# Masked attention and an int8 linear layer on one core: PSUM tiles taken by threes, v and q in other portions, the second-last linear layer moved behind the last scores

## The chip, the core and the metric

The kernel runs on 1 of the 8 cores of a Trainium2 chip. The metric is device time in microseconds (us); the time before is 2547.27 us, the median of 3 runs (2547.04 to 2548.92). TensorE is called PE, VectorE DVE, ScalarE ACT, GpSimd POOL and SyncE SP, as in the profile. PE works out of SBUF into PSUM; DVE and ACT read PSUM; POOL works on SBUF alone. Each engine runs its instructions in the order of the program and waits on semaphores of the others.

## The reference, cut to what matters

```python
# x: (8, 512, 1024) f32, mask: (8, 1024); 16 heads of 32 channels
Q, K, V = (proj(Wq), proj(Wk), proj(Wv))          # each (B, H, T, Dh) from x (B, C, T)
att = jnp.einsum('bhqd,bhkd->bhqk', Q, K) * (1.0 / math.sqrt(Dh))
att = att + b[0]
att = att * m + (1.0 - m) * NEG_INF
att = jax.nn.softmax(att, axis=-1)
y = jnp.einsum('bhqk,bhkd->bhqd', att, V)         # back to (B, C, T)
...
q, in_scale = per_token_quant_int8(y)             # one scale for each row of T values
acc = jnp.einsum('bsk,nk->bsn', q, weight, preferred_element_type=jnp.int32)
out = acc.astype(jnp.float32) * in_scale * w_scale[:, 0] + bias
return x + out.astype(jnp.float16)
```

So each batch has 16 heads with 1024 x 1024 scores, and the linear layer sees each channel's 1024 values over T as one row.

## The kernel before

**Groups, halves, steps, pairs.** The 8 x 16 heads are taken as 32 groups `i` of four heads (128 channels; four groups to a batch). A group has two halves of 512 queries (`X = 2i + h`), and a half has 8 steps of 128 keys (`s`, 512 in all). The main loop runs over pairs `n` of two steps: 8 pairs to a group (`p` = 0 to 7), 256 in all, and five pairs ahead of them (`n` = -5 to -1, `i` = -1, `p` = 3 to 7) that only prepare. All five engines are scheduled by hand: an engine's order is the order of the calls.

**What a step does.** `scores` (L408) writes the scores of four heads, keys by queries, into two PSUM tiles of two banks each: L419 puts in the negated maximum of each query (`shift`), L424 adds k times q. ACT takes the exponential (L433) into a tile `e` of SBUF, of which there are three. `product` (L451, its matmuls L458) multiplies `e` with v into one bank (`ps_av`); after 8 steps ACT copies that to `y` (L468). `add_up` (L438) sums the `e` of a half on POOL (L445), and ones-matmuls turn the sum into the denominators (`half_denominators` L478, `add_rows` L472). For the last 12 steps (`s >= ON_ARRAY`) there is no sum on POOL: `last_denominators` (L488) feeds every `e` to the ones-matmuls (L474) as it comes, and a copy (L504) brings the result to SBUF. `normalise` (L506) takes four reciprocals (L511) and one product (L514).

**Maxima.** The maximum of each query over its unmasked keys has to be known before the scores that are exponentiated. `maxima` (L335) computes the scores of 128 queries against 1024 keys of one head into a PSUM tile of two banks, from `stacks` in which q and k stand as high and low halves (L345), and DVE reduces it (L376). Each pair of steps works off four such units, five pairs ahead; the first eight units of all are `first_maxima` (L354), from the unsplit q and k. `split_tops` on POOL (L393 to L397) and a DMA transpose on SP (L402) make `shift` of eight units' worth of maxima and more: once per half, at the start of the pair before the half's first scores are due.

**PSUM.** Eight banks: two tiles of two banks under `ps_s`, one of two banks under `ps_m`, one bank `ps_av`, one bank `ps_job`. Scores take both `ps_s` tiles in every step. `maxima_bank` (L330) lets unit `k` use `ps_s` where `k % 4` is 1 or 2 and `ps_m` otherwise, so that the units follow each other as m, s, s, m, m, s, s, m.

**Jobs.** Beside that, `job` (L690) hands every pair a list of pieces that use the one bank `ps_job`: `project` (L199) makes q or k of a half of a coming group, as a rule as 8 matmuls of 256 columns (two quarters by four chunks `c` of 128 input channels); where `(i + 2) % 4 == 0`, and `p` = 4, as 4 matmuls of 512 columns, so that the last q of a batch gives its chunks of `x` free one by one. `project_v` (L281) makes v in quarters of two key tiles; `linear` (L622) is the int8 layer, half an output at a time. `evict` (L230) splits q and k into high and low with two ACT instructions and, by way of `later`, one of DVE at the end of the pair. The main loop (L818 to L892) puts the first piece, cut into columns (L197), between the two steps if the list has 8 pieces or `p` is 4, and spreads the others over the four units of maxima; behind the first unit only if more than 4 are left (L888).

**The opening.** `first_projections` makes k and half of q of group 0 from `x` as its chunks land, k ahead of q in each chunk; then the five pairs `n` = -5 to -1 make, by turns, v's first four key tiles, the rest of q, v's other four, and group 1's q and k. `after_units` issues on SP the DMAs that fill the stacks (`stack_head` L316, four DMAs to each call).

**The end.** In group 31 `quantise` (L546) rounds group 30's `y` on ACT, in four steps between the exponentials (L554 to L560); group 30's linear layer runs on PE between the last steps (`open_linear`, `run_linear`, L858 to L880). After the loop come the normalisation, the scale, the rounding (`round_half`) and the linear layer of group 31 (`last_linear` L572), and `add_residual` (L614), whose two additions for each half (L618, L619) run on POOL, or for the very last half on DVE, ahead of the store (L620).

Of the kernel before, what the change touches and what calls it, by code (L numbers as in the profile page):

```python
# [20 lines left out]
P = 128  # L21
# [11 lines left out]
def kernel(  # L33
# [50 lines left out]
    ON_ARRAY = n_steps - NT - HN  # L84
    SCALE = 1.0 / math.sqrt(DH)
# [113 lines left out]
    def project(i, which, h, quarters=(0, 1), width=QUARTER):  # L199
# [4 lines left out]
        def piece(a, c, matmul=nc.tensor.matmul):  # L204
            acc = jobs["bank"]
            cols = slice(a * width, (a + 1) * width)
            place = slice((a - quarters[0]) * width, (a - quarters[0] + 1) * width)
# [4 lines left out]
                start=(c == 0),  # L212
                stop=(c == NG - 1),
            )
            if (a, c) == (quarters[-1], NG - 1):
                cols = slice(quarters[0] * width, (a + 1) * width)
                evict(i, which, h, cols, acc[:, : place.stop])

        return [lambda *x, a=a, c=c: piece(a, c, *x) for a in quarters for c in range(NG)]
# [31 lines left out]
    def first_projections():  # L251

        pair = ps_s.tile([P, NH, HALF], F32, tag="s", name="kps_0")
        accs = [(1, 0, pair[:, 0, :]), (1, 1, pair[:, 1, :]), (0, 0, bank("qps_0"))]
        for c in range(NG):
            for which, h, acc in accs:
                nc.tensor.matmul(
                    acc,
                    w_qk[0, which][:, c, :],
                    x_sb[0, c][:, h * HALF : (h + 1) * HALF],  # L260
                    start=(c == 0),
                    stop=(c == NG - 1),
                )
# [10 lines left out]
        for which, h, acc in accs:  # L274
# [6 lines left out]
    def project_v(i, quarters):  # L281
# [4 lines left out]
        def piece(a, r, matmul=nc.tensor.matmul):  # L286
# [5 lines left out]
            place = (k - quarters[0] * KQ) * P  # L292
# [8 lines left out]
            if (a, r) == (quarters[-1], 2 * KQ - 1):  # L301
                nc.scalar.copy(  # L302
                    v_sb[i][:, quarters[0] * KQ : (a + 1) * KQ, :].rearrange("p k c -> p (k c)"),
                    acc[:, : place + P],
# [11 lines left out]
    def stack_head(i, j, which, h):  # L316
# [4 lines left out]
        for a, part in enumerate(order):  # L321
            nc.sync.dma_start(  # L322
# [7 lines left out]
    def maxima_bank(k):  # L330

        pool, tag = (ps_s, "s") if k % HN in (1, 2) else (ps_m, "m")
        return pool.tile([P, NH, HALF], F32, tag=tag, name=f"mps_{k}")
# [74 lines left out]
    def scores(s):  # L408
# [7 lines left out]
        accs = [ps_s.tile([P, 2, HALF], F32, tag="s", name=f"sps_{s}_{a}") for a in range(2)]  # L416
# [71 lines left out]
    def last_denominators(s):  # L488
# [5 lines left out]
        if X not in last_sums:  # L494
            if whole:
                last_sums[X] = ps_m.tile([P, HALF], F32, tag="m", name=f"dps_{X}")
            else:
                last_sums[X] = bank(f"dps_{X}")
                add_rows(last_sums[X], sums[X], True, False)
        acc = last_sums[X]  # L500
        add_rows(acc, exps[s], whole and kc == 0, kc == NT - 1)
        if kc == NT - 1:
            dens[X] = work.tile([P, HALF], F32, tag="den", name=f"den_{X}")
            nc.vector.tensor_copy(dens[X], acc)  # L504

    def normalise(X, step):  # L506
        i, h = divmod(X, NH)
        d = dens[X]
        if step < HN:
            piece = d[:, step * P : (step + 1) * P]  # L510
            nc.vector.reciprocal(piece, piece)  # L511
# [34 lines left out]
    def quantise(i, step):  # L546
# [5 lines left out]
        y = ys[i]  # L552
        if step == 1:
# [18 lines left out]
    def last_linear(i):  # L572
# [12 lines left out]
        accs = [bank(f"job_{i}"), ps_m.tile([P, HALF], F32, tag="m", name=f"job_{i}_1")]  # L585
# [19 lines left out]
    def load_residual(i, h):  # L605
        b, g = divmod(i, NG)
        half = slice(h * HALF, (h + 1) * HALF)
        xr = work.tile([P, HALF], F32, tag=f"xr{h}", name=f"xr_{i}_{h}")
        nc.sync.dma_start(xr, x[b, g * P : (g + 1) * P, half])
        o = work.tile([P, HALF], F32, tag=f"o{h}", name=f"o_{i}_{h}")  # L610
# [79 lines left out]
    def job(i, p):  # L690
# [4 lines left out]
        if i < 0:  # L695
            if p in (3, 5):
                return project_v(0, (0, 1) if p == 3 else (2, 3))
            if p == 4:
                return project(0, 0, 1)
            return project(1, p - 6, 0)  # L700
# [4 lines left out]
        if p == 4:  # L705

            by_chunk = dict(quarters=(0,), width=HALF) if (i + 2) % NG == 0 else {}
            return project(i + 1, 0, 1, **by_chunk)
# [4 lines left out]
        if p in (1, 2):  # L713
            pieces += project_v(i + 1, (a,))
# [4 lines left out]
    def after_units(i, p):  # L719

        flush(stores)
        if i == last:
# [3 lines left out]
            if p == 3:  # L726
                quantise(i - 1, 0)
            if p == 5:
                turn(i - 1)
                for step in range(5):  # L730
                    normalise(2 * i, step)
        elif group(i - 1):
# [223 lines left out]
```

## Time and profile before

| | us |
|---|---|
| median of 3 runs | 2547.27 |
| the profiled execution | 2548.53 |
| its span, first to last instruction | 2546.7 |
| PE busy | 2502.2 (98%) |
| POOL busy | 2244.9 (88%) |
| DVE busy | 1799.6 (71%) |
| ACT busy | 1479.0 (58%) |
| first scores (n = 0) begin | 58.11 |
| pair n = 1 begins | 69.46 |
| pair n = 4 begins | 98.97 |
| pair 0 of group 31 begins | 2457.00 |
| pair 4 of group 31 begins | 2495.35 |
| last matmul of the last product ends | 2527.28 |

A time in a stage is counted from the span's start. A pair begins with the first L419 matmul of its first step. An f32 matmul shows as two records in the trace, so `x8` of L424 are the four matmuls of a step. Matmuls of different 32-row or 32-column strips run beside each other, so a group's wall time is not the sum of its records.

### The profile page before, as it was taken

To read this page: it belongs to the slowest core of one execution; us is meant where nothing else is said; L and a number is where in the kernel's file an instruction comes from. 1 tells how busy PE (TensorE), PEld (TensorE's weight loads), DVE (VectorE), ACT (ScalarE), POOL (GpSimd) and SP (SyncE) were. 2 spreads that over 40 slices of the span, in tenths; PEclk is the share of its full clock that TensorE was granted. 3 is DMA by queue.
4 is the path that set the end of the run, shared out by engine and by line. 5 is a ranking of instruction groups with operands and counts; after the bars stand their busy time and mean duration, and the time that the engine had idled before them with its cause. 6 is when DMAs were issued, how large, how long until landed. Compare 5 with 4: busy or idle time off the path is not lost.

```text
span 2546.7 us, 50694 instructions
## 1 busy us (share of the span) xinstructions
PE 2502.2 (98%) x19364; PEld 1417.0 (56%) x19364; DVE 1799.6 (71%) x2893; ACT 1479.0 (58%) x1657; POOL 2244.9 (88%) x909
## 2 busy tenths in 40 slices
PE   7999999999999999999999999999999999999997
PEld 4555555555555555555555555655555555555532
DVE  4567677777777777777777777777777777777764
ACT  2456665566665556655556665566655566555554
POOL 1889899999999999999999999999999998999991
PEclk9999999999999999999999999999999999999999
DMA  4423433333333433334333343333433334333321
GB/s 126 109 67 80 125 74 85 80 105 100 88 83 82 118 84 89 81 92 113 79 84 94 81 119 78 79 86 96 115 85 75 85 96 112 84 81 79 79 71 44
DMA packets 225951, 228.08 MB, mean 90 GB/s; under 512 B 104368, under 2 KB 138160, under 8 KB 225712
## 3 DMA queue, kind: packets, MB, share of 16 engines
q1 hardware_dynamic: 225712, 224.85, 34.4%
q8 instruction: 155, 2.54, 0.4%
q14 instruction: 84, 0.69, 0.1%
HBM read 57.70 MB, written 16.78 MB: 29 GB/s over the span
## 4 chain that ended last, share of the span: by engine, by line
PE 80%; POOL 13%; issue 2%; ACT 1%; SPq 1%; DMA 1%; DVE 1%; POOLq 0%; DVEq 0%; ACTq 0%
PE mps L345 17%; PE av L458 15%; PE sps L424 14%; PE job L208 13%; POOL sum L445 11%; PE job L294 7%; PE sps L419 6%; PE job L635 3%; PE dps L474 2%; PE job L197 2%; ACT e L433 1%; SPq L322 1%; POOL o L619 1%; POOL o L618 1%; POOL part L395 0%
## 5 line engine op out<-in xcount | busy, mean ns | idle before, releaser
L445 POOL TENSOR_TENSOR sum<-sum,e 128x2048 f32<-128x2048 f32 x374 | 1707.9, 4567 | 30.5 <-ACT e L433 11.3
L376 DVE CUSTOM_DVE_ANT_0 rest<-mps,row 128x1024 bf16<-128x1024 f32 x1024 | 1253.3, 1224 | 608.7 <-PE mps L345 362.8
L433 ACT ACTIVATE e<-sps,kbias 128x1024 f32<-128x1024 f32 x1024 | 1085.7, 1112 | 453.2 <-PE sps L424 421.1
L345 PE MATMUL mps<-ks,qs 128*128 128x512 f32 x2032 | 766.7, 458 | 16.1 <-ACT e L433 12.7
L424 PE MATMUL sps<-qf,kf 32*128 32x512 f32 x4096 | 550.4, 589 | 0.0
L458 PE MATMUL av<-e,v 128*32 128x512 f32 x4096 | 493.4, 598 | 0.0
L345 PEld LDWEIGHTS mps<-ks,qs 128*128 128x128 f32 x2032 | 332.4, 190 | 253.1 <-DVE den L484 93.3
L445 POOL TENSOR_TENSOR sum<-e,e 128x2048 f32<-128x2048 f32 x63 | 286.3, 4544 | 149.4 <-ACT e L433 144.4
L458 PEld LDWEIGHTS av<-e,v 128*32 128x32 f32 x4096 | 107.5, 109 | 346.4 <-issue 346.1
L294 PEld LDWEIGHTS job<-wv,x 128*128 128x128 f32 x1860 | 255.1, 191 | 27.2
L294 PE MATMUL job<-wv,x 128*128 128x128 f32 x1860 | 257.1, 274 | 0.0
L208 PE MATMUL job<-x,wq 128*128 128x256 f32 x850 | 241.5, 390 | 0.0
L419 PE MATMUL sps<-shift,ones_b 32*128 32x512 bf16 x2048 | 229.4, 383 | 4.7 <-DVE tops L376 3.0
L511 DVE RECIPROCAL den<-den 128x128 f32<-128x128 f32 x256 | 228.3, 924 | 0.0
L208 PE MATMUL job<-x,wk 128*128 128x256 f32 x854 | 223.8, 378 | 0.0
L424 PEld LDWEIGHTS sps<-qf,kf 32*128 32x128 f32 x4096 | 207.5, 183 | 4.3
L302 ACT COPY v<-job 128x256 f32<-128x256 f32 (+1 forms) x93 | 41.3, 444 | 252.5 <-PE job L294 252.5
L208 PEld LDWEIGHTS job<-x,wk 128*128 128x128 f32 x854 | 161.2, 189 | 30.7
L208 PEld LDWEIGHTS job<-x,wq 128*128 128x128 f32 x850 | 160.2, 188 | 32.3
L419 PEld LDWEIGHTS <-ones_b 32*128 32x128 bf16 x2048 | 70.1, 91 | 189.8 <-issue 172.6
L237 ACT ACTIVATE qh<-job,top 128x256 fp32r<-128x256 f32 (+1 forms) x91 | 49.7, 547 | 177.1 <-PE job L208 151.8
L635 PE MATMUL job<-w_sb,qT 128*128 128x256 bf16 (+1 forms) x944 | 126.4, 276 | 0.0
(101 smaller groups left out, 1440.2 us busy)
## 6 DMA issues: line engine op xcount, KB each, us to landing
ks<-kh SPq DMA_DIRECT2D x512, 64.0 KB, 2.0
ks<-kl SPq DMA_DIRECT2D x512, 64.0 KB, 2.0
qs<-qh SPq DMA_DIRECT2D x508, 64.0 KB, 2.0
qs<-ql SPq DMA_DIRECT2D x508, 64.0 KB, 2.0
x<-in_x SPq DMA_DIRECT2D x32, 512.0 KB, 4.4
xr<-in_x SPq DMA_DIRECT2D x64, 256.0 KB, 3.5
out<-o SPq DMA_DIRECT2D x64, 256.0 KB, 3.4
wk<-in_wkT SPq DMA_DIRECT2D x32, 256.0 KB, 3.7
```

The costliest lines, as they stand in the source:

```text
L197: nc.tensor.matmul(acc[r : r + DH], weights[:, r : r + DH], moving, **kwargs)
L208: matmul(acc[:, place], w[:, c, :], x_sb[b, c][:, h * HALF : (h + 1) * HALF][:, cols], start=(c == 0), stop=(c == NG - 1),)
L294: matmul(acc[:, place : place + P], x_sb[b, c][:, k * P : (k + 1) * P], wv_sb[:, c, g * P : (g + 1) * P], start=(c == 0), stop=(c == NG - 1),)
L345: nc.tensor.matmul(acc[:, a, :], q[:, n0 * P : (n0 + 1) * P], kk[:, a * HALF : (a + 1) * HALF], start=True, stop=True,)
L376: nc.vector.tensor_tensor_reduce(out=rest, in0=acc.rearrange("p h t -> p (h t)"), in1=row, scale=-1.0, scalar=HIGH, op0=ALU.add, op1=ALU.m ...
L419: nc.tensor.matmul(accs[j // 2][:, j % 2, :], ones_b[r, :], shift[r, :], start=True, stop=False)
L424: nc.tensor.matmul(accs[j // 2][:, j % 2, :], k[r, k0 * P : (k0 + 1) * P], q[r, :], start=False, stop=True,)
L433: nc.scalar.activation(e[:, 2 * a : 2 * a + 2, :], acc, AF.Exp, bias=kbias[:, kc : kc + 1], scale=SCALE)
L445: nc.gpsimd.tensor_tensor(sums[X], other, exps[s], ALU.add)
L458: nc.tensor.matmul(accs_av[X][r, :], v_sb[i][:, kc, r], exps[s][:, j, :], start=(kc == 0), stop=(kc == NT - 1),)
L511: nc.vector.reciprocal(piece, piece)
L635: matmul(acc, qT[:, k, :], w8_sb[:, k, half][:, cols], start=(k == 0), stop=(k == NT - 1),)
```

## The change

The diff has six parts. The opening's maxima take `ps_s`, `ps_m`, `ps_s` by threes instead of m, s, s, m, and so do the scores from step 502 on. In the opening q's second half comes first, in portions of four pieces, v's first half follows, and v's second half moves into pairs 1 and 2 of group 0, in one bank with group 1's v; the jobs of `n` = -3 and -1 use `ps_av`; one stack is issued by ACT's queue and k's second stack three pairs earlier. The last q of a batch is made in 8 pieces of 256 columns, chunk by chunk, instead of 4 of 512, and for group 31 in the usual order. Group 30 is rounded on DVE. Its linear layer moves behind the last product, with its results finished inside `last_linear`. The last denominators lie in `ps_job` and are read there by the reciprocals, without a copy, and the maximum of the first half of group 31 is taken in pair 5.

```diff
+    BY_TURNS = n_steps - NT - 2
...
-    def project(i, which, h, quarters=(0, 1), width=QUARTER):
+    def project(i, which, h, quarters=(0, 1), by_chunk=False):
...
-                start=(c == 0),
-                stop=(c == NG - 1),
+                start=(c == 0 and (a == 0 or not by_chunk)),
+                stop=(c == NG - 1 and (a == quarters[-1] or not by_chunk)),
...
-        return [lambda *x, a=a, c=c: piece(a, c, *x) for a in quarters for c in range(NG)]
+        order = [(a, c) for a in quarters for c in range(NG)]
+        if by_chunk:
+            order.sort(key=lambda o: o[1])
+        return [lambda *x, a=a, c=c: piece(a, c, *x) for a, c in order]
...
     def first_projections():
-        pair = ps_s.tile([P, NH, HALF], F32, tag="s", name="kps_0")
-        accs = [(1, 0, pair[:, 0, :]), (1, 1, pair[:, 1, :]), (0, 0, bank("qps_0"))]
...
+        k0, k1 = (ps_s.tile([P, HALF], F32, tag="s", name=f"kps_0_{h}") for h in range(NH))
+        accs = [(0, 0, bank("qps_0")), (1, 0, k0), (1, 1, k1)]
+        order = [(c, a) for c in range(NG - 1) for a in accs[1:] + accs[:1]]
+        order += [(NG - 1, a) for a in accs]
...
-    def project_v(i, quarters):
+    def project_v(i, quarters, offset=0):
...
-            place = (k - quarters[0] * KQ) * P
+            place = offset + (k - quarters[0] * KQ) * P
...
-    def stack_head(i, j, which, h):
+    def stack_head(i, j, which, h, engine=nc.sync):
...
-            nc.sync.dma_start(
+            engine.dma_start(
...
-        pool, tag = (ps_s, "s") if k % HN in (1, 2) else (ps_m, "m")
+        first = k < -FIRST * HN
+        pool, tag = (ps_s, "s") if (k % 3 != 1 if first else k % HN in (1, 2)) else (ps_m, "m")
...
-        accs = [ps_s.tile([P, 2, HALF], F32, tag="s", name=f"sps_{s}_{a}") for a in range(2)]
+        for a in range(2):
+            third = s >= BY_TURNS and (2 * (s - BY_TURNS) + a) % 3 == 2
+            pool, tag = (ps_m, "m") if third else (ps_s, "s")
...
         if X not in last_sums:
-            if whole:
-                last_sums[X] = ps_m.tile([P, HALF], F32, tag="m", name=f"dps_{X}")
-            else:
-                last_sums[X] = bank(f"dps_{X}")
+            last_sums[X] = bank(f"dps_{X}")
+            if not whole:
                 add_rows(last_sums[X], sums[X], True, False)
...
-            nc.vector.tensor_copy(dens[X], acc)
+            if not whole:
+                nc.vector.tensor_copy(dens[X], acc)
...
-            nc.vector.reciprocal(piece, piece)
+            source = last_sums[X] if X == n_halves - 1 else d
+            nc.vector.reciprocal(d[:, cols], source[:, cols])
...
     def quantise(i, step):
...
+        if i == last - 1:
+            if step == 1:
+                nc.vector.tensor_scalar(y, y, inv, ROUND, ALU.mult, ALU.add)
+            elif step == 2:
+                nc.vector.tensor_scalar(y, y, ROUND - 128.0, ROUND + 127.0, ALU.max, ALU.min)
+            else:
+                nc.vector.tensor_scalar(qt, y, -ROUND, None, ALU.add)
+            return
...
     def last_linear(i):
...
-        accs = [bank(f"job_{i}"), ps_m.tile([P, HALF], F32, tag="m", name=f"job_{i}_1")]
+        flush(later)
+        accs = [
+            pool.tile([P, HALF], F32, tag=tag, name=f"job_{i}_{h}")
+            for h, (pool, tag) in enumerate(((ps_m, "m"), (ps_s, "s")))
+        ]
...
+    def linear_before_last(i):
+        qT, scale = outs.pop(i)
+        accs = [ps_av.tile([P, HALF], F32, tag="av", name=f"job_{i}_0"), bank(f"job_{i}_1")]
+        for h, acc in enumerate(accs):
+            for k in range(NT):
+                nc.tensor.matmul(
+                    acc,
+                    qT[:, k, :],
+                    w8_sb[:, k, h * HALF : (h + 1) * HALF],
+                    start=(k == 0),
+                    stop=(k == NT - 1),
+                )
+        def rest():
+            for h, acc in enumerate(accs):
+                half = slice(h * HALF, (h + 1) * HALF)
+                nc.vector.scalar_tensor_tensor(
+                    residual[i, h][1], acc, scale, ws_sb[:, half], ALU.mult, ALU.mult
+                )
+                add_residual(i, h, nc.gpsimd)
+            flush(stores)
+        later.append(rest)
...
-    def load_residual(i, h):
+    def load_residual(i, h, tiles=None):
...
         if i < 0:
-            if p in (3, 5):
-                return project_v(0, (0, 1) if p == 3 else (2, 3))
-            if p == 4:
-                return project(0, 0, 1)
-            return project(1, p - 6, 0)
+            if p < HP + 1:
+                if p == HP - 1:
+                    jobs["first"] = project(0, 0, 1)
+                return [jobs["first"].pop(0) for _ in range(NG)]
+            return project_v(0, (0, 1)) if p == 5 else project(1, p - 6, 0)
...
-            by_chunk = dict(quarters=(0,), width=HALF) if (i + 2) % NG == 0 else {}
-            return project(i + 1, 0, 1, **by_chunk)
+            return project(i + 1, 0, 1, by_chunk=group(i + 2) and (i + 2) % NG == 0)
...
         if p in (1, 2):
+            if i == 0:
+                pieces = project_v(0, (NH + a,), QUARTER)
             pieces += project_v(i + 1, (a,))
...
         if i == last:
...
-            if p == 3:
-                quantise(i - 1, 0)
+            if p == 4:
+                for step in range(4):
+                    quantise(i - 1, step)
             if p == 5:
                 turn(i - 1)
                 for step in range(5):
                     normalise(2 * i, step)
+                tops_y.append(largest(i, 0))
+                for h in range(NH):
+                    load_residual(i - 1, h)
...
         if i < 0 and p == 3:
...
-            for j in (2, 3):
+            for j, engine in ((2, nc.sync), (3, nc.scalar)):
                 for which, h in ((1, 0), (1, 1), (0, 0)):
-                    stack_head(0, j, which, h)
+                    stack_head(0, j, which, h, engine)
+            for h in range(NH):
+                stack_head(0, 0, 1, h)
...
             for j in range(HG if i >= 0 else 1):
-                if i < 0:
-                    for h in range(NH):
-                        stack_head(0, j, 1, h)
                 stack_head(i + 1, j, 0, 1)
+            if i < 0:
+                for h in range(NH):
+                    stack_head(0, 1, 1, h)
...
-            last_denominators(a)
-            product(a)
+            order = (product, last_denominators)
+            for what in order if a == n_steps - NT else order[::-1]:
+                what(a)
...
             if n == -1:
-                for h in range(NH):
-                    stack_head(0, 1, 1, h)
                 for j in range(1, HG):
                     stack_head(0, j, 0, 1)
...
         if pieces:
-            jobs["bank"] = bank(f"job_{n}")
-        if n == n_pairs - 1:
-            open_linear(last - 1, 1)
-            run_linear(2)
+            if n < 0 and n % 2 and n > FIRST:
+                jobs["bank"] = ps_av.tile([P, HALF], F32, tag="av", name=f"job_{n}")
+            elif n != FIRST + 1:
+                jobs["bank"] = bank(f"job_{n}")
...
-            if len(pieces) == 2 * NG or (pieces and p == HP):
+            if len(pieces) == 2 * NG:
                 pieces.pop(0)(columns)
...
-            if n == n_pairs - 2:
-                open_linear(last - 1, 0)
-                run_linear(4)
-            if n == n_pairs - 1:
-                run_linear(2)
...
-            if a > 0 or len(pieces) > NG:
+            if a > 0 or len(pieces) > NG or n < 0:
...
+    spare = epool.tile([P, HG, HALF], F32, tag="e", name="spare")
+    for h in range(NH):
+        load_residual(last, h, (spare[:, h, :], spare[:, NH + h, :]))
     sum_up(n_steps)
-    tops_y = [largest(last, 0)]
-    flush(finishes)
-    flush(stores)
-    for h in range(NH):
-        load_residual(last, h)
+    linear_before_last(last - 1)
     for step in range(5):
         normalise(2 * last + 1, step)
```

## The prediction

> **What bounds the kernel now.** First the page's busy times.
>
> ```profile
> PE 2502.2 (98%) x19364; PEld 1417.0 (56%) x19364; DVE 1799.6 (71%) x2893; ACT 1479.0 (58%) x1657; POOL 2244.9 (88%) x909
> ```
>
> PE sets the pace, so what counts is PE work taken away and the few places where PE stands. I found those by reading the start of the first L419 record of each pair. A pair takes 9.38 to 9.91 us by its place in the group, 77.08 us a group, with no idle PE. Three places fall out: pair 4 of groups 2, 6, 10, 14, 18, 22, 26 and 30 (10.58 to 10.59 us instead of 9.78), the opening (98.97 us up to pair 4 of group 0), and the end from step 502 on. Next, PE's timeline (start, time, line, records, idle before and what ended it) of pair 4 in group 6, and of the same pair in group 7.
>
> ```profile
> 562.97 0.40 PE L419 MATMUL sps<-shift,ones_b 32*128 32x512 bf16 x4
> ...
> 565.89 1.04 PE L197 MATMUL job<-x,wq 128*32 128x512 f32 x8
> ...
> 569.39 0.74 PE L345 MATMUL mps<-ks,qs 128*128 128x512 f32 x2 [0.52 <-ACT e L433]
> ...
> 573.56 0.40 PE L419 MATMUL sps<-shift,ones_b 32*128 32x512 bf16 x4
> ```
>
> ```profile
> 640.85 0.40 PE L419 MATMUL sps<-shift,ones_b 32*128 32x512 bf16 x4
> ...
> 643.77 0.61 PE L197 MATMUL job<-x,wq 128*32 128x256 f32 x8
> ...
> 650.64 0.39 PE L419 MATMUL sps<-shift,ones_b 32*128 32x512 bf16 x4
> ```
>
> 10.59 against 9.79 us. With 512 columns the piece in columns is 0.43 us longer, and as only three pieces are left, none stands between the first two units of maxima: PE waits 0.52 us there for the exponentials to free a `ps_s` tile. Then PE's timeline of the opening.
>
> ```profile
> 19.48 1.99 PE L363 MATMUL mps<-kf,qf 32*128 32x512 f32 x8 [1.92 <-ACT qf L269]
> ...
> 29.65 1.99 PE L363 MATMUL mps<-kf,qf 32*128 32x512 f32 x8 [0.71 <-DVE tops L376]
> ...
> 38.17 0.74 PE L345 MATMUL mps<-ks,qs 128*128 128x512 f32 x2 [0.77 <-DVE tops L376]
> 39.54 1.16 PE L294 MATMUL job_-3_301<-wv,x 128*128 128x128 f32 x8 [0.63 <-DVE ql L243]
> ...
> 53.07 1.13 PE L208 MATMUL job_-1_401<-x,wk 128*128 128x256 f32 x4 [0.92 <-DVE ql L243]
> ...
> 58.11 0.40 PE L419 MATMUL sps<-shift,ones_b 32*128 32x512 bf16 x4
> ...
> 64.41 0.70 PE L345 MATMUL mps<-ks,qs 128*128 128x512 f32 x2 [1.59 <-DMA qs<-ql]
> ```
>
> PE waits for DVE because two units in a row take the one `ps_m` tile, and for `ql` because there is one job bank. DVE in turn idles 2.76, 2.07 and 1.23 us before units 2, 4 and 6, since PE puts 16 matmul records of v or 8 of q between two doubles. Last the end: all engines' timeline.
>
> ```profile
> 2526.49 0.69 DVE L504 COPY den<-dps 128x512 f32<-128x512 f32 x1
> ...
> 2527.10 0.67 DVE L523 TENSOR_REDUCE ytop<-y 128x1 f32<-128x512 f32 x1
> ...
> 2527.70 3.38 DVE L511 RECIPROCAL den<-den 128x128 f32<-128x128 f32 x4
> ...
> 2534.21 1.23 PE L581 MATMUL qtps<-ident,qt 128*128 128x128 bf16 x8 [6.92 <-DVE qt L544]
> ...
> 2541.44 1.49 POOL L619 TENSOR_TENSOR o<-o,xr 128x512 f32<-128x512 f16 x1
> 2541.94 1.53 DVE L619 TENSOR_TENSOR o<-o,xr 128x512 f32<-128x512 f16 x1
> 2542.95 0.89 SPq L620 DMA_DIRECT2D out<-o  x2
> ```
>
> PE stands 6.92 us there while DVE works alone, and 3.46 us of group 30's linear layer (L197, 32 + 16 + 16 records at 1.73, 0.86, 0.86 us) were done just before, on PE's busy path.
>
> **The change, part by part** (minus is faster).
>
> *q by chunks in eight pieces.* Seven groups (2 to 26) get the list length, the columns and the spreading of an ordinary pair 4: 7 x (10.585 - 9.78) = -5.6. The order by chunk costs nothing in itself, as every matmul loads its weights anyway (PEld 56% busy, hidden). The cover to watch is `x`: chunk 2 is given back at the third unit, as before, and SP's next load waits in any case for `wq`, which the pair's last piece frees. Bounds 0 and -5.7.
>
> *Group 30* makes q the usual way: PE gains 0.8, but from 2426.8 on POOL's sums follow each other with gaps of 0.08 up to the split of the maxima at 2452.5 that pair 0 of group 31 needs. That chain starts at an `e` which moves only by the shorter piece in columns, 0.42. I take -0.4 (bounds 0, -0.8).
>
> *The opening.* With q first, ACT's `qf` (0.68) starts at 18.27 instead of 18.74, and the first maxima at 19.0 instead of 19.48. DVE starts 2.1 later (19.48 to 21.62) and takes 1.375 a unit (21.62, 22.99). With three tiles by turns, a double of maxima waits only for the unit three before its second, and two pieces of q (0.86) lie between doubles instead of four of v: DVE begins units 0, 2, 4, 6 at 21.1, 24.6, 28.1, 31.6 and ends unit 7 at 34.4 (38.1 before). Then `ql` 0.7, and units 8 to 15 without a gap, as three tiles and the second job bank take away the waits: 35.1 + 8 x 1.375 = 46.1 (51.4 before). PE needs 0.57 + 0.81 = 1.38 a unit there, no more than DVE. The first scores need `ps_s` from units 17 and 18: 46.1 + 0.7 + 3 x 1.375 = 50.9 against 58.11, -7.2; the maxima's transpose is there, 4.2 after unit 15 (51.36 to 55.56) at 50.3. In pair 0 the 1.59 for `qs` goes, since SP has no k stack (8 DMAs, 4.9 us) left ahead of it; the 0.7 for `kl` gives nothing, because the wait for `e` behind it ends at the same time. -8.8. Pairs 1 and 2 take four more pieces of v each (1.75): they become like pair 3, about 10.0 instead of 9.25 and 9.41, +1.3; the 0.74 for `shift` in pair 3 is covered by them, as POOL's chain (25.9 us from 73.02 to 98.97) starts with step 2's `e` and moves along. Together -8.3 at pair 4.
>
> Unknown here is the clock. The windows view grants 0.51 from 21.9 to 25.4, after PE had idled 1.92 us; idle stretches of 1.59 us and less (62.8 to 64.4) left it whole. Now the stretch is 1.45, nearer to the second, so I count on the full clock; if it falls all the same, the second double ends 1.5 later, -6.8. The Trainium skill, "TensorE: Matmul & The Clock Gate", section "What's actually happening", lets the clock fall only after a whole idle window of about 3.4 us; this trace differs, since 1.92 us went before the fall. By that rule the term would be -8.3 as well. Bounds -5 (clock low, and ACT's queue somewhat late) and -9.5.
>
> ACT issues 12 of the DMAs: at SP's median of 0.59 us they run from 21.1, behind the casts, to 28.2, while ACT's next work, q's eviction, is due at 32.4. So they cost nothing up to 0.94 us each. Stack 2 is issued by SP by 28, as before.
>
> *The end.* A step there is scores 1.18 (0.23 + 0.96 in undisturbed pairs), dps 0.86 and av 0.86, 2.9 together; the trace has 3.35 (2505.91, 2509.26, 2512.61), because both `ps_s` tiles wait for ACT, which was also rounding group 30 (4 x 1.15). With three tiles scores wait only for the first half of the step before, which is 1.1 us of ACT behind 1.72 of PE, and ACT needs 2.12 a step. From 2495.35: 8 x 1.18 + 7 x 1.72 = 2516.8, then `e` of the last step 2.2, dps 1.0: 2520.1 against 2526.43, -6.3, the linear layer's 3.46 in it. On DVE the copy and the early maximum go (2526.49 to 2527.70): -1.2. DVE's rounding of group 30, about 4.5 us, hides in 14.81 us of idle before 2517.86. From the first reciprocal to `qt` stays 6.46, so `qt` is at 2526.7. The linear layer moved there fits under it: eight matmuls after `y` is copied (2521.5), eight after the reciprocals (2523.5), done by 2525.3, or 2527 at half clock. But its four additions now stand on POOL before group 31's: first result 2.5 after `qt`, then 2 x (1.27 + 1.16 + 0.16) = 5.2 and 2.7 for the last: `qt` + 10.4, where DVE's chain ended at `qt` + 9.31 before. What is late next is the store: +1.1, plus 0.45 as the last one is issued behind POOL's. -6.3 - 1.2 + 1.5 = -6.0. Bounds -4 (only half of the shorter steps) and -8.7 (no queue on POOL, clock full).
>
> Sum: -8.3 - 5.6 - 0.4 - 6.0 = **-20.3**. The profiled execution took 2548.53 (span 2546.7, 1.8 around it), 1.26 above the median; it would be 2528.2, the median 2527.0.
>
> **The rivals.**
>
> *The steps at the end stay at 3.35*, because ACT sets them: 8 x 0.45 comes back, 2530.6. For it: ACT's `e` ended PE's waits there. Against: 2.12 a step once the rounding is gone. 10%.
>
> *Pair 4 doesn't shorten*, the change not doing what it says, because PE still waits for `e` between units: 2532.6. Against: 9.78 in all other groups with the same list. 6%.
>
> *Group 0 holds the opening's gain back*: POOL's casts wait for the w8 loads, which had landed at 80.75, 1.4 before POOL came. If these move 5 less than POOL: 2532. Against: SP has 8 DMAs less ahead of them. 4%.
>
> *Slower*: ACT's queue. Each issue above 0.94 us delays q's eviction, `ql` behind it on DVE, and unit 8 behind that, 12 times over. SP's longest issue was 2.0: 12.7 late, 2539.7, still faster. From 2.6 each it eats all, and at 3.0 the time is 2551.7. Against: the median 0.59. 3%.
>
> **How the numbers follow.** Forecast 74%, the rivals 10, 6, 4 and 3, and 3% for gains that cancel out. 0.2% (5.1 us) is about what can be told from no change: faster 0.94, within 0.03, slower 0.03. The bounds add up to -14.0 and -24.7, that is 2533.3 to 2522.6, and hold the first three rivals: 2522 to 2533.5.
>
> **What would show it.** Right: pair 4 at 9.8 in group 6; no L345 wait for L376 before 46; first L419 near 51, pair 4 of group 0 near 90.7; steps of 2.9 at the end; no L504 for the last half; POOL's L619 as the last work. Wrong: ACT's DMA issues reaching past 32, waits for `e` in group 6, or steps above 3.2.

## The result and the profile after

The changed kernel takes 2532.97 us, the median of 4 runs (2532.84 to 2533.22), against 2547.91 (2547.04 to 2548.92, 4 runs) for the kernel before: ratio 0.9943, 95% interval 0.9931 to 0.9956, 14.9 us less by the medians and 11 to 18 by the interval, where 20.3 were forecast. Its profiled execution took 2533.22 (span 2531.4). Each stage, as the difference of the two profiled executions (a pair begins with the first matmul of `shift`, now L432):

| stage | forecast | measured |
|---|---|---|
| opening, up to pair 4 of group 0 | -8.3 | -9.11 |
| pair 4 of groups 2, 6, ..., 26 | -5.6 | 7 x -0.35 = -2.43 |
| pair 4 of group 30 | -0.4 | -0.80 |
| pair 4 of group 31 to the end | -6.0 | -5.26 |
| every other pair | 0 | +2.29 (pair 7 of group 1 alone +1.15) |
| sum | -20.3 | -15.3 |

First the busy times on the page: PE is busy for 4.1 us less, so most of the gain is waits.

```profile
PE 2498.1 (99%) x19404; PEld 1429.0 (56%) x19404; DVE 1804.9 (71%) x2895; ACT 1475.1 (58%) x1654; POOL 2244.1 (89%) x909
```

PE's timeline of pair 4 in group 6 (start, time, line and operation, idle before and what ended it), and then ACT's at the same place:

```profile
554.61 0.40 PE L432 MATMUL sps<-shift,ones_b 32*128 32x512 bf16 x4
...
557.53 0.61 PE L198 MATMUL job<-x,wq 128*32 128x256 f32 x8
558.08 0.91 PE L432 MATMUL sps<-shift,ones_b 32*128 32x512 bf16 x4
558.60 1.24 PE L437 MATMUL sps<-qf,kf 32*128 32x512 f32 x8
...
564.85 0.39 PE L432 MATMUL sps<-shift,ones_b 32*128 32x512 bf16 x4
```

```profile
554.71 0.59 ACT L309 COPY v<-job 128x512 f32<-128x512 f32 x1 [3.09 <-PE job L301]
555.19 1.15 ACT L188 ACTIVATE row<-mask,nb 128x1024 bf16<-128x1024 f32 x1
556.24 0.29 ACT L189 ACTIVATE kbias<-kbias,nb 128x8 f32<-128x8 f32 x1
556.43 2.11 ACT L446 ACTIVATE e<-sps,kbias 128x1024 f32<-128x1024 f32 x2
```

The piece in columns is down to 0.61 and the 0.52 wait between the units is gone, but the pair lasts 10.24, not 9.78. The second step's four L432 take 0.91 where an undisturbed pair has 0.40, with no idle time listed: half of them wait inside the group. ACT has just spent 1.44 on the mask of the next batch, which is prepared in these very groups, so the first `e` starts late and frees its tile late. Before, the longer piece of q covered that.

PE's timeline of the opening and of pair 1 of group 0:

```profile
18.45 1.99 PE L372 MATMUL mps<-kf,qf 32*128 32x512 f32 x8
20.36 1.13 PE L210 MATMUL job_-5_179<-x,wq 128*128 128x256 f32 x4
21.42 2.28 PE L372 MATMUL mps<-kf,qf 32*128 32x512 f32 x8
...
49.08 0.40 PE L432 MATMUL sps<-shift,ones_b 32*128 32x512 bf16 x4 [1.72 <-DMA shift<-part]
...
66.44 0.71 PE L301 MATMUL job<-wv,x 128*128 128x128 f32 x4 [0.46 <-ACT v L309]
```

No unit waits for DVE any more, and the one wait left before the first scores is for the transpose of the maxima. In pairs 1 and 2 PE stands 0.46 for the copy of group 0's piece of v out of the bank that group 1's v goes on filling.

PE's timeline of the end, then POOL's and DVE's:

```profile
2494.41 0.40 PE L432 MATMUL sps<-shift,ones_b 32*128 32x512 bf16 x4
2494.64 1.03 PE L437 MATMUL sps<-qf,kf 32*128 32x512 f32 x8
2495.59 1.06 PE L487 MATMUL dps<-e,ones_f 128*32 128x512 f32 x8
2496.47 1.04 PE L471 MATMUL av<-e,v 128*32 128x512 f32 x8
2497.45 0.40 PE L432 MATMUL sps<-shift,ones_b 32*128 32x512 bf16 x4
...
2512.69 3.84 PE L639 MATMUL job<-w_sb,qT 128*128 128x512 bf16 x16 [0.68 <-ACT y L481]
2517.73 0.40 PE L604 MATMUL qtps<-ident,qt 128*128 128x128 bf16 x4 [1.20 <-DVE qt L558]
...
2518.64 3.63 PE L616 MATMUL job<-w_sb,qT 128*128 128x512 bf16 x16
```

```profile
2519.95 1.27 POOL L675 TENSOR_TENSOR o<-o,bias_sb 128x512 f16<-128x512 f32 x1 [40.40 <-DVE o L650]
...
2523.75 1.16 POOL L676 TENSOR_TENSOR o<-o,xr 128x512 f32<-128x512 f16 x1
...
2526.21 1.49 POOL L676 TENSOR_TENSOR spare<-o,spare 128x512 f32<-128x512 f16 x1
```

```profile
2511.20 3.39 DVE L525 RECIPROCAL den<-dps 128x128 f32<-128x128 f32 x4 [14.33 <-PE dps L487]
...
2516.72 0.49 DVE L557 TENSOR_SCALAR y<-y,inv 128x512 f32<-128x512 f32 x1
2517.25 0.43 DVE L558 TENSOR_SCALAR qt<-y 128x512 bf16<-128x512 f32 x1
...
2524.95 1.73 DVE L675 TENSOR_TENSOR o<-spare,bias_sb 128x512 f16<-128x512 f32 x1 [1.89 <-POOL o L676]
2526.71 1.53 DVE L676 TENSOR_TENSOR spare<-o,spare 128x512 f32<-128x512 f16 x1
```

A step of the last half goes from 2494.41 to 2497.45, 3.04 us, with no wait. The linear layer of group 30 fills PE's gap under DVE's chain. The clock, at half from 2530.7 to 2537.5 in the profile before, where PE had stood, stays full here under the last linear layer: its sixteen matmuls (L616) take 3.63 instead of 4.71. Six additions stand on POOL, one behind the other. DVE's last two begin when the fourth of them ends, since they write the f16 tile which that one reads, and they are the last work, over at 2528.24, 0.54 behind POOL's.

### The profile page after: what moved, and what is told of

The parts are those of the page before. It is cut to its first block, busy times and chain, and to the rows that moved or that the text cites. A ratio compares the mean times of both kernels' runs of the same rounds, so it can differ in the third digit from the quotient of the medians.

```text
span 2531.4 us, 50774 instructions
## 1 busy us (share of the span) xinstructions
PE 2498.1 (99%) x19404; PEld 1429.0 (56%) x19404; DVE 1804.9 (71%) x2895; ACT 1475.1 (58%) x1654; POOL 2244.1 (89%) x909
## 4 chain that ended last, share of the span: by engine, by line
PE 57%; POOL 34%; issue 6%; ACT 1%; DVE 0%; DMA 0%; SPq 0%; POOLq 0%; DVEq 0%
POOL sum L458 29%; PE mps L354 12%; PE av L471 10%; PE sps L437 10%; PE job L210 9%; PE job L301 5%; PE sps L432 4%; PE job L692 2%; POOL o L676 2%; POOL o L675 1%; PE dps L487 1%; PE job L198 1%; ACT e L446 1%; POOL part L404 1%; POOL tops L406 1%
## 5 line engine op out<-in xcount | busy, mean ns | idle before, releaser
L432 PE MATMUL sps<-shift,ones_b 32*128 32x512 bf16 x2048 | 229.0, 383 | 8.3 <-DVE tops L385 4.1
L210 PEld LDWEIGHTS job<-x,wq 128*128 128x128 f32 x914 | 172.3, 189 | 34.2
L432 PEld LDWEIGHTS <-ones_b 32*128 32x128 bf16 x2048 | 69.6, 91 | 186.4 <-issue 167.7
```

The costliest lines, as they stand in the source:

```text
L210: matmul(acc[:, place], w[:, c, :], x_sb[b, c][:, h * HALF : (h + 1) * HALF][:, cols], start=(c == 0 and (a == 0 or not by_chunk)), stop=( ...
L432: nc.tensor.matmul(accs[j // 2][:, j % 2, :], ones_b[r, :], shift[r, :], start=True, stop=False)
```

## The experiments

Each changes the kernel named by the few lines shown. "Changed" is the kernel after the change. Where two pairs are compared, both are of profiled executions.

**Each part alone on the kernel before.** Three kernels, each with one of the diff's groups of edits: q by chunks; the end; the opening.

```diff
+            return project(i + 1, 0, 1, by_chunk=group(i + 2) and (i + 2) % NG == 0)
```

> The kernel before with one part of the change alone: the last q of a batch in 8 pieces of 256 columns, chunk by chunk. Theory: pair 4 goes from 10.585 to 10.24 in seven groups and to 9.78 in group 30, where no mask is prepared: -0.35 x 7 - 0.8 = -3.2 us, 2544.7. The prediction's own price would be -5.6 - 0.4 = -6.0, 2541.9.

2546.98 (ratio 0.9995, interval 0.9986 to 1.0005): within what can be told from no change. Span -1.9. Pair 4 is 0.35 shorter in six groups and 0.80 in group 30. In group 18 pair 3 ran 0.53 late and pair 4 then gained the whole 0.80: a delay ahead of the pair covers the mask just as the long piece did.

```diff
+    BY_TURNS = n_steps - NT - 2
...
+    linear_before_last(last - 1)
```

> The kernel before with the part of the change that concerns the end alone: scores by threes from step 502 on, group 30 rounded on DVE, its linear layer behind the last product, denominators read from PSUM, the early maximum. Theory: the profile of the changed kernel shows this part as it is: steps of 3.04 us instead of 3.35 and more, and -5.3 us from pair 4 of group 31 to the end: about 2542.6. Rival: part of it came from the other parts (a kernel that arrives earlier at the end is in another clock window): then less than -4.

2542.49 (0.9979, 0.9969 to 0.9988), span -6.2: from pair 4 of group 31 on -0.86, -0.90, -2.35 and -1.16, together -5.27, as in the changed kernel. The other 1.07 lie in the opening, ahead of everything the edit touches. In the profile before the clock was at half from 21.9 to 25.4; in this execution, and in that of q by chunks, it stayed full there. The sixteen matmuls of v behind the first double took 2.05 instead of 3.31, and pair 4 of group 0 begins at 97.90 (q by chunks: 97.72) instead of 98.97, although the first maxima began later (20.00 against 19.48).

```diff
+        first = k < -FIRST * HN
+        pool, tag = (ps_s, "s") if (k % 3 != 1 if first else k % HN in (1, 2)) else (ps_m, "m")
...
+            for j, engine in ((2, nc.sync), (3, nc.scalar)):
```

> The kernel before with the opening of the change alone (tiles by threes for the first maxima, q ahead of v, v's second half in group 0, two job banks, one stack on ACT's queue). Theory: the gain of 9.1 us at pair 4 of group 0 that the changed kernel's profile shows stays to the end, within 1.5 us for the moment at which the mask lands (14.40 in the profile before, 12.91 after): 2537.3 to 2540.3. Rival: a part of it is lost again in groups 0 and 1, where POOL's sums set the pace: -7 or less, 2541.

2542.42 (0.9976, 0.9967 to 0.9985), span -6.9: -9.36 up to pair 4 of group 0, of which 2.4 are lost again later, 0.94 in pair 7 of group 1. That is nearer to the rival's -7 than to the theory, though pair 7's loss is a late transpose (below) and not POOL's sums. In their own stages the parts alone gave what they give together: -2.88 and -0.81, -5.27, -9.36, against -2.43, -0.80, -5.26 and -9.11. So the parts don't touch each other, and where the forecast is short it is short inside a part. That the three spans also add up to -15.0, near the -15.3 of all parts at once, is luck, since the first two hold 1.24 and 1.07 of the full clock in the opening; by the medians the parts add up to -12.9, against -14.9.

**The order of the pieces of q**, on the changed kernel.

```diff
-            return project(i + 1, 0, 1, by_chunk=group(i + 2) and (i + 2) % NG == 0)
+            return project(i + 1, 0, 1, by_chunk=False)
```

> The changed kernel, but the last q of a batch in the usual order, quarter by quarter, in all groups. In the changed kernel pair 4 of groups 2 to 26 takes 10.24 us where it was costed at 9.78. Theory: the 0.46 us come from ACT, which works off the next batch's mask row (1.15 us) at the start of that pair, so that the exponentials free the scores' tiles late; the order of the pieces has no part in it. Then pair 4 stays at 10.2. Rival: the order by chunk itself costs 0.46 (matmuls to and fro between two quarters of a bank); then pair 4 falls to 9.8 and the time by 7 x 0.46 = 3.2 us, to about 2529.8. By both, x's last chunk is given back later here: its chunks load behind the end of pair 4 (three loads of 4.4 us, partly beside each other), and pair 5, which needs the last one about 4.5 us after its start, may stand for up to 5 us in each of the seven groups, 35 us in all.

2533.48 (2533.44 to 2533.85), pair 4 still 10.24 in all seven groups, and pair 5 unchanged. So the order by chunk is not what holds pair 4 at 10.24; it isn't needed either, as no wait for `x` came.

**The mask's steps in the middle of pairs 1, 2 and 3**, on the changed kernel.

```diff
-                if 1 <= p < 4:
-                    prepare_mask(b + 1, p - 1)
...
+            if a == 1 and 1 <= p < 4 and group(i + 1):
+                b, g = divmod(i + 1, NG)
+                if g == NG - 1 and b + 1 < B:
+                    prepare_mask(b + 1, p - 1)
```

> The changed kernel with the three steps that prepare a batch's mask moved ahead by half a pair: behind the second unit of maxima of pairs 1 to 3 instead of the end of these pairs, where ACT is idle for about 3 us. Theory: the mask's ACT work at the start of pairs 3 and 4 costs 0.24 and 0.46 us in seven groups; then pair 4 falls from 10.24 to 9.8, pair 3 from 10.13 to 9.9, and the time by 7 x 0.70 = 4.9 us, to about 2528.1. Rival (order by chunk): pair 4 stays at 10.24 and only pair 3 gains, 7 x 0.24 = 1.7 us, 2531.3.

2536.36 (2536.0 to 2537.5), slower by 3.4. Pair 4 fell to 9.78 in all seven groups and pair 3 by 0.21, so ACT's work on the mask is what they lost; but pair 2 became 1.08 longer. DVE's timeline of this kernel at the turn of pair 1 to pair 2, and PE's:

```profile
534.37 1.22 DVE L176 TENSOR_REDUCE top<-mask 128x1 f32<-128x1024 f32 x1
535.62 0.15 DVE L178 TENSOR_SCALAR less<-top 128x1 f32<-128x1 f32 x1
535.69 1.22 DVE L385 CUSTOM_DVE_ANT_0 rest<-mps,row 128x1024 bf16<-128x1024 f32 x1
```

```profile
535.81 0.39 PE L432 MATMUL sps<-shift,ones_b 32*128 32x512 bf16 x2
536.97 0.39 PE L432 MATMUL sps<-shift,ones_b 32*128 32x512 bf16 x2 [0.77 <-DVE tops L385]
```

The first step of the mask, a row maximum on DVE, now stood ahead of the pair's last units of maxima, and the scores of pair 2 waited for their tile. At the end of pair 1 it lies in DVE's idle time.

**Maxima of the opening as m, s, s, m again**, on the changed kernel.

```diff
-        first = k < -FIRST * HN
+        first = False
```

> The changed kernel, but the opening's maxima take their tiles by fours again (m, s, s, m). Theory: most of the opening's gain is the third tile: DVE's chain of 20 units gets back the waits of the kernel before (2.07, 1.23 and 0.57 us ahead of units 4, 6 and 9, 0.82 ahead of unit 12), and the first scores come 3 to 4 us later: 2536 to 2537. Rival: the gain comes from the shorter jobs between the first maxima and from the second job bank; then under 1.5 us is lost.

2541.32 (2536.47 to 2542.09, 6 runs): the first scores start 8.41 later. PE's timeline and the windows view (stretch, busy time of PE, PE's loads, DVE, ACT and POOL, granted clock, DMA):

```profile
26.84 2.10 PE L372 MATMUL mps<-kf,qf 32*128 32x512 f32 x8 [1.34 <-DVE tops L385]
...
30.88 3.78 PE L372 MATMUL mps<-kf,qf 32*128 32x512 f32 x8
```

```profile
28.60:42.20 13.60, 12.91 (x36) 8.00 (x35) 7.85 (x12) 1.27 (x2) 0.00 (x0) 0.50 0.41 103
```

The waits for the tile themselves (1.34, 0.69, 0.45 and 0.62) are about 3.1, and 0.74 is a later start of the first maxima in this execution (19.19 against 18.45). The rest, some 4.6, is put down to the clock, at half for 13.6 us. The one execution without it, by its mean clock (0.999, the others 0.996), took 2536.47, 3.5 more than the changed kernel.

**All stacks on SP's queue**, on the changed kernel.

```diff
-            for j, engine in ((2, nc.sync), (3, nc.scalar)):
+            for j, engine in ((2, nc.sync), (3, nc.sync)):
```

> The changed kernel with all stacks issued by SP, as before the change. Theory: ACT's queue saves SP 12 issues of 0.6 us; without that the stack of head 3 is there at about 36 instead of 29, and the unit that needs it first (unit 12) runs on PE at 36.2, so the loss lies between 0 and 2 us there, and SP's later stacks (k of heads 0 and 1) come 7 us later, at about 49, ahead of their use at 41.6 (head 0, unit 16): up to 5 us lost: 2533 to 2538. Rival: SP has room, nothing changes: 2533.0.

2542.75 (2540.45 to 2543.5), 9.8 slower: more than was expected. PE's timeline and SP's issues of this kernel, and SP's issue of the same load in the changed one:

```profile
38.38 0.71 PE L354 MATMUL mps<-ks,qs 128*128 128x512 f32 x2 [1.73 <-DMA qs<-ql]
45.16 2.08 PE L210 MATMUL job_-2_330<-x,wq 128*128 128x256 f32 x4 [6.08 <-DMA wq<-in_wqT]
```

```profile
41.91 0.53 SPq L117 DMA_DIRECT2D wq<-in_wqT  x1
```

```profile
33.75 0.53 SPq L117 DMA_DIRECT2D wq<-in_wqT  x1
```

The twelve issues hold up not only their own stack (1.73) but the load of `wq` queued behind them, by 8.16, for which PE stands 6.08, from 39.09 on. The clock is at half from 40.9, within that wait, to 51.2. Without the move to ACT's queue pair 4 of group 0 begins at 100.38, later than before the change (98.97), though the prediction spoke only of what the move might cost. But without the tiles by threes it begins at 98.53: the opening's gain needs both, and isn't the share of one.

**The last scores with two tiles again**, on the changed kernel.

```diff
-    BY_TURNS = n_steps - NT - 2
+    BY_TURNS = n_steps
```

> The changed kernel with two tiles for the scores up to the end. Theory: with two tiles scores wait for the exponentials of the step before; without ACT's rounding a step of the kernel before took 3.24 us (2512.61 to 2515.85), against 3.04 with three: 9 steps x 0.2 = 1.8 us, 2534.8. Rival: the third tile makes the whole difference to 3.35 to 3.5: 9 x 0.4 = 3.6 us, 2536.6; or nothing, 2533.0, if PE's work alone sets the step.

2536.67 (2535.61 to 2537.2); pairs 4 to 7 of group 31 +0.86, +0.75, +0.75 and +0.92, together +3.3. PE's timeline:

```profile
2496.35 0.77 PE L432 MATMUL sps<-shift,ones_b 32*128 32x512 bf16 x4
2496.74 1.24 PE L437 MATMUL sps<-qf,kf 32*128 32x512 f32 x8
...
2499.77 0.77 PE L432 MATMUL sps<-shift,ones_b 32*128 32x512 bf16 x4
```

A step is 3.42 though the rounding is on DVE: with two tiles the scores wait for ACT in each step, whether it rounds or not. The third tile makes the shorter steps.

**Group 30 rounded on ACT again**, on the changed kernel.

```diff
-        if i == last - 1:
+        if False:
...
+            if i == last and p in (4, 5):
+                quantise(i - 1, 2 * p - 7)
```

> The changed kernel with group 30 rounded on ACT between the exponentials, as before. Theory: ACT needs 2.12 + 1.15 = 3.27 us in each of four steps, more than PE's 3.04, and with three tiles the step goes to about 3.3: 4 x 0.25 = 1.0 us, 2534.0. Rival: three tiles cover it and nothing changes, 2533.0, or the rounding was what held the steps at 3.35 and more before: 4 x 0.4 = 1.6 us, 2534.6.

2534.09 (2533.35 to 2534.7), +1.1; pair 4 of group 31 alone is longer, by 0.91.

**Group 30's results on ACT and POOL, the first half early**, on the changed kernel.

```diff
+            nc.scalar.activation(o, accs[h], AF.Copy, scale=scale)
+            nc.gpsimd.tensor_tensor(o, o, ws_sb[:, half], ALU.mult)
...
+        rest(0)
+        later.append(lambda: rest(1))
```

> The changed kernel, with group 30's results taken from PSUM by ACT (a copy with the row's scale) instead of DVE, and multiplied by the weights' scale on POOL, the first half before group 31's normalisation instead of within its linear layer. Theory: in the changed kernel the end is set by POOL, which works off six additions one after the other from 2519.95 to 2527.70; with the first half out of the way by 2519, POOL is ready for group 31 at about 2522.6, when its result comes (2522.2), and the end comes 2 to 2.6 us earlier: 2530.4 to 2531.0. Rival: PE's last linear layer and DVE set the end: under 0.7 us.

2534.26 (2531.26 to 2535.58, 4 runs): not settled. The four ran at mean clocks of 0.997, 0.997, 1.0 and 0.998, and the one at 1.0 took 2531.26. The windows view of the profiled execution shows half clock in the middle of the last linear layers, and DVE's and POOL's timelines what came before:

```profile
2519.20:2526.00 6.80, 5.92 (x20) 2.56 (x21) 1.58 (x3) 0.39 (x1) 4.26 (x4) 0.50 0.20 77
```

```profile
2517.45 1.19 DVE L557 TENSOR_SCALAR y<-y,inv 128x512 f32<-128x512 f32 x1
2518.67 1.27 DVE L558 TENSOR_SCALAR qt<-y 128x512 bf16<-128x512 f32 x1
```

```profile
2517.09 1.26 POOL L675 TENSOR_TENSOR o<-o,bias_sb 128x512 f16<-128x512 f32 x1
2518.43 1.22 POOL L676 TENSOR_TENSOR o<-o,xr 128x512 f32<-128x512 f16 x1
```

Besides the clock the edit has a price of its own, in this profile and at full clock in the next kernel's: POOL now works while DVE makes `qt`, and the two instructions take 1.19 and 1.27 instead of 0.49 and 0.43, each ending 0.29 behind the addition beside it; a small one ahead of them takes 0.52 instead of 0.16. From the first reciprocal to `qt` it is 8.38, not 6.48. That POOL's work slows DVE here is read from these rows; no run separates it. Half clock from 2447.5 to 2450.9 made pair 0 of group 31 longer by 1.38 as well, in this execution and in that of the pieces quarter by quarter.

**The mask in mid pair, the edit just shown, and the copy of group 0's piece of v at the pair's end, together.** The last of the three is:

```diff
-                nc.scalar.copy(
...
+                if offset:
+                    later.append(copy)
+                else:
+                    copy()
```

> The changed kernel with three edits together: the mask's steps in the middle of pairs 1 to 3, group 30's results through ACT and POOL, and in pairs 1 and 2 of group 0 the copy of group 0's v at the end of the pair, since the copy in its middle holds the next matmul to the same bank for 0.46 us. Theory: -4.9, -2.3 and -2 x 0.46 = -0.9: about 2524.9. If the order by chunk costs, and not the mask: 2528.

2535.44 (2532.91 to 2536.06): a miss. Pairs 1 and 2 of group 0 gained 0.72 each, but the mask's row maximum cost pair 2 of seven groups 1.08 as above. In the profiled execution, at a mean clock of 1.0, the stretch from pair 7 of group 31 to the end is 27.27 against 27.90 in the changed kernel: so the edit of group 30's results was worth 0.63 there, not 2 to 2.6.

**The mask's two steps on ACT in mid pair, its maximum where it was, v's copy at the pair's end**, on the changed kernel.

```diff
-                if 1 <= p < 4:
-                    prepare_mask(b + 1, p - 1)
+                if p == 1:
+                    prepare_mask(b + 1, 0)
...
+            if a == 1 and 2 <= p < 4 and group(i + 1):
```

> The changed kernel with two corrections: the mask's two steps on ACT are issued in the middle of pairs 2 and 3 instead of at the pairs' ends, while its first step (the row maximum on DVE) stays at the end of pair 1; and in pairs 1 and 2 of group 0 the copy of group 0's piece of v is issued at the end of the pair, behind that of group 1's piece. Theory (pair 2 lost 1.08 us in the kernel with all three steps moved because the row maximum, 1.2 us on DVE, then stood ahead of the last maximum of the pair, for which the scores wait; the steps on ACT are what pairs 3 and 4 lose in seven groups; the early copy of v is what pairs 1 and 2 of group 0 lose): pair 2 as in the changed kernel, pair 3 -0.21 and pair 4 -0.46 in seven groups, 7 x 0.67 = -4.7; pairs 1 and 2 of group 0 -0.72 each, as in the kernel that had it with other parts; total -6.1, some 2526.8 us. Rival (the loss of pair 2 was ACT's first step in mid pair, not DVE's): pair 2 stays +1.08, total +0.4 x 7 - 1.45 = +1.4, some 2534.3 us.

2526.79 (2525.89 to 2527.17, 5 runs; ratio to the kernel before 0.9916, 0.9902 to 0.993), 6.2 less than the changed kernel, the fastest here. In the seven groups pair 2 is unchanged, pair 3 -0.21, pair 4 -0.46; pairs 1 and 2 of group 0 -0.72 and -0.74. PE's timeline of pair 4 in group 6:

```profile
556.05 0.45 PE L438 MATMUL sps<-shift,ones_b 32*128 32x512 bf16 x4
556.28 1.08 PE L443 MATMUL sps<-qf,kf 32*128 32x512 f32 x8
```

The second step's `shift` takes 0.45 instead of 0.91. The rival, that ACT's first step in mid pair 2 was the loss, falls.

## Why the prediction was right, and where it was off

The time is 2532.97, inside the range, but 0.5 below its upper end and some 6 above the forecast. The mechanisms are those the prediction gave; the sizes were off.

*q by chunks in eight pieces: -2.4, not -5.6.* The step that failed is "Seven groups (2 to 26) get the list length, the columns and the spreading of an ordinary pair 4". The list was ordinary, but the pair wasn't: ACT's 1.44 on the mask falls at its start, and 0.46 of it had been covered by what was taken away. The forecast named covers for `x` and for the order, and none for ACT. The comparison with pair 4 of group 7 could not show this, since group 7 prepares no mask. The profile before showed the mask's cost one pair earlier: pair 3 takes 10.13 to 10.15 in just these seven groups and 9.90 to 9.92 in others, which the prediction's "9.38 to 9.91 us" passes over. The last experiment got the 7 x 0.46 back.

*Group 30: -0.8, not -0.4.* It prepares no mask, so the whole 0.80 is there, and POOL's chain towards group 31, which was to take half, took nothing.

*The opening: -9.1, not -8.3.* Two errors partly cancel here, and part of the surplus is luck. The -9.1 is counted from a profile with the clock at half from 21.9 to 25.4; from the two executions of the old opening with a full clock it is about 8.0. And the mask landed at 12.91 instead of 14.40, so that DVE began unit 0 at 20.4 (forecast 21.1) and the idle stretch of 1.45 that the forecast kept ahead of the first maxima wasn't there; with the mask at 14.26, in the last experiment, the first scores came only 0.37 later. What was mis-sized is the wait of a double: the forecast let the second begin when DVE had done unit 0, at 22.5, but its first unit had a free tile and it began at 21.42, with no idle. So DVE began units 2, 4 and 6 at 23.4, 26.7 and 29.7 (forecast 24.6, 28.1 and 31.6). Unit 15 ended at 43.9 instead of 46.1, and the first scores came at 49.08 instead of 50.9; the limit there is now the transpose, not the `ps_s` tile. Pairs 1 and 2 took back 2.5 rather than 1.3: the forecast made them 10.0 each by pair 3's pattern, they are 10.56 and 10.62, and 0.72 of each goes when the copy of v is issued later. The clock stayed full, as chosen. "So they cost nothing up to 0.94 us each" holds, with issues of 0.52 to 0.85 on ACT.

*The end: -5.3, not -6.0.* The step was 3.04 instead of 2.9: dps 0.88 and av 0.98 where 0.86 was taken for each. Seven such steps lie ahead of the last scores, and 7 x 0.14 = 1.0 is most of what the first reciprocal is later than forecast (25.91 after pair 4 begins, by the forecast 24.75). From there to `qt` it is 6.48 (forecast 6.46), and from `qt` to the end 13.75 (14.05). So POOL's queue costs about what was said, but by holding up DVE's last additions: these, and not POOL's, are the last work.

*Everything else: +2.3, forecast 0.* Half of it is pair 7 of group 1. The view of one line for the 64 transposes of `shift`, in the changed kernel and then in the one before:

```profile
L411 SPq DMA_TRANSPOSE shift<-part x64: 1200/1225/1879, 45.6 to 2479.6; - x64
...
DMA to landing us min/median/max: 2.4/2.5/4.4
```

```profile
DMA to landing us min/median/max: 2.4/2.5/4.1
```

The transpose in that pair took 4.4 us to land, and the scores behind it started 1.08 late. The kernel before has late ones too (4.1), but not where scores wait that long for them. The pair is longer in every kernel with the new opening, or most of it (+0.74 to +1.65), and in neither of the two without it. What slows the transpose was not tried. The rest is 0.2 to 0.4 in single pairs, to both sides, whose causes stay open.

Of the rivals, steps of 3.35 came only when the third tile was taken away (3.42). *Pair 4 doesn't shorten* came half true, by another wait: for `e` ahead of the second step's scores, not between the units. Group 0 held nothing back: its pairs 3 to 7 (9.88, 9.78, 9.31, 9.52, 9.89) take what group 1's took before the change. ACT's queue cost nothing.

## What to carry to other kernels

When a piece of work on the critical engine is made shorter, list what else falls into that place in the program, on every engine, in exactly those iterations: an iteration without that work is no model for them. A transfer's issue delays all that is queued behind it, so a move between queues is priced by the loads that come forward, not by its own issue time. Work that is moved earlier has to go in behind what the next stage waits for, as the row maximum showed: the same instruction cost 1.08 us or nothing by its place in DVE's order.

## What was not expected of the hardware

PE's clock can make small waits dear: in the opening with the maxima as m, s, s, m, 1.34 us of idle PE was followed by 13.6 us at half clock, worth some 4.9 us (2541.4 against 2536.47). The Trainium skill, "TensorE: Matmul & The Clock Gate", section "What's actually happening", puts the fall after a whole idle window of about 3.4 us. The end of the kernel before agrees: PE was idle for all of the 3.40 us ahead of the fall at 2530.7. This opening differs: in the 3.40 us ahead of the fall, still at full clock, PE was busy for 2.06, and with all stacks on SP for 0.71. Nor does the length of a wait settle it: 1.72 us of idle ahead of the first scores of the changed kernel left the clock whole.

Issuing twelve transfers of 0.6 us from another engine was worth 9.8 us. The Trainium skill, "DMA: Bandwidth & Descriptors", section "Issuing engines are not separate DMA queues", says that this saves only the sequencer's time, usually small beside the transfer. The trace agrees on what is saved, 8.16 us of SP's time, and one issue is small beside its transfer (a median of 0.59 us against 2.0 to landing in the profile before); but twelve of them were not small for the load behind them, which PE needed.
